# Mask parts in one run of fetches, and loads and sources issued in another order, in a two-layer graph-attention kernel

## The chip, the cores and the metric

One Trainium2 chip, of which one core runs the kernel. The metric is the time of one execution on the device, in microseconds (us); lower is better. Engines: TensorE (PE; its weight loads are PEld), VectorE (DVE), ScalarE (ACT), GpSimd (POOL), and SyncE (SP), which here only issues DMA transfers.

## The reference, cut to what matters

`x` is (8, 2048, 256) in float32, `adj` (2048, 2048) of 0 and 1 in int32. Two layers, each with a residual:

```
h = relu(layernorm(x))
q, k, v = h Wq^T + bq, h Wk^T + bk, h Wv^T + bv        # 4 heads of 64
s = clip(q k^T / 8, -10, 10); s = where(adj == 0, -10, s)
a = softmax of s within each chunk of 256 keys (8 chunks)
x = x + layernorm(sum over the chunks of a v, times Wo^T, + bo + h) * gamma + beta

h = relu(layernorm(x));  q = h W                       # 4 heads of 64
e = leaky_relu(q a_src [row] + q a_dst [column], 0.2)
x = x + elu(softmax(where(adj > 0, e, -9e15)) q)       # over all 2048 columns
```

## The kernel before, in words

**Layer 0** runs over 256 steps: 8 batches, 4 blocks of 512 queries, 8 chunks of 256 keys (the loop at line 731; its counter stands in `here[0]`). A step has two key tiles. Its contexts (line 460) take the weights that were made two steps before; its scores (line 440 on PE) are those of two steps ahead. DVE clips and masks a score tile (line 448, with `limit`, which holds the mask), ACT takes the exponential (line 454), POOL adds the two key tiles (line 725), and PE adds up over the keys (line 471). The sums then go a long way: ACT copies them (line 478), SP spreads them over the partitions by a DMA (line 480), DVE takes the reciprocal (line 485), SP writes it to memory and reads it back four times (lines 487 and 490), and DVE multiplies the contexts by it (line 498). POOL adds that to what earlier chunks gave (line 500).

**The order is written out by hand.** Each engine runs its instructions in the order of the program, and SP's queue is in order too: a transfer whose buffer isn't free holds up whatever stands behind it. In a step the program has: the first half of the contexts, the first `advance()`, four score tiles (the exponentials of the first two after them), the sums of the next step, their copy and its DMA, the other exponentials and POOL's additions, the second half of the contexts, the accumulation, the reciprocal with its DMAs, and the second `advance()`.

`aside` is a list of generators that hold all other work in pieces. `advance()` (line 212) goes through the list: a generator that yields `True` or `False` lets the next one have its turn, one that yields `None` has done a heavy piece, and the call ends there. Before step 0 such a generator also goes to the end of the list. `later()` (line 198) yields `False` until `here[0]` has grown. `drain(until)` calls `advance` until a condition holds. `quiet` has generators that `tick` moves in every round: `finish` (line 502: output projection, second layernorm, and the DMA of the result to memory from POOL's queue, line 553) and the statistics of the next batch.

**The mask** comes in 32 parts: 4 query blocks, 4 row tiles each, 2 halves of 1024 columns. For a part, SP loads 128 x 1024 int32 (line 251; three buffers `adj_in`), ACT casts it to bfloat16 (line 257), DVE takes the smallest value (line 258), PE transposes it in eight (line 272), and DVE makes `limit` of it (line 273). `make_limit(qb)` (line 244) does the eight parts of one query block, with three fetches at its start; `other_limits` runs it for blocks 1, 2 and 3 and joins `aside` at step 0. Scores of a block can't be issued before its mask is there (line 714), so a block that is not done is made in a `drain`. The rest of `aside` at that time is the first batch: `batch` and `block` (turning h by PE transposes, lines 144 to 164, and projections to k, v and q with PE at line 153).

**The change of layers.** `last_batch` makes batch 7 of layer 0, then runs `sources_of` (line 567) and `preparation(0)` (line 588), both in `aside`, while layer 0 still works on its last batch. `sources_of` multiplies W by the two attention vectors: four times a product on POOL (line 579) and its sum on DVE (line 583), with a `yield True` between. `preparation(b)` loads the four blocks of `x1` (the result of layer 0, in memory; line 110 through `ahead`), one ahead of use, makes h, turns it, gets the attention terms `er` (line 606), writes them to memory (line 622) with their extremes (`ends`, line 624), reads the extremes of all partitions back (`gm`, line 626), and later makes the projection qn.

**Layer 1** has 32 passes (8 batches, 2 pairs of heads, 2 halves of the rows) of 16 rounds (the loop at line 903; `here[0]` grows once in four rounds). At the start of a pass ACT makes `near` (line 798) from `es`, two rows that `sources` (line 779) reads back from memory with a DMA to all partitions; DVE makes e (line 809), PE the products (line 820) and sums (line 832), ACT and POOL pair the tiles for the sums (lines 924 and 928). `es` of the next pass is loaded in round 2 or 8; that of the first pass after the `drain` at line 890, right ahead of the loop. Preparation of the next batch and the `ending` of a pass run in `aside`.

Of the kernel before, what the change touches and what calls it, by code (L numbers as in the profile page):

```python
# [16 lines left out]
P = 128  # L17
# [34 lines left out]
def layers(  # L52
# [54 lines left out]

    def load(rows, blk):
        xb = big.tile([P, NT, F], F32, tag="x", name="x", bufs=3)
        nc.sync.dma_start(xb, rows[blk * QB : (blk + 1) * QB, :].rearrange("(t p) f -> p t f", p=P))  # L110
        return xb

    def ahead(rows):

        coming = load(rows, 0)
        for blk in range(NQB):
            xb = coming
            if blk + 1 < NQB:
                coming = load(rows, blk + 1)
            yield xb  # L120
# [77 lines left out]
    def later():  # L198
        n = here[0]
        while here[0] < n + 1:  # L200
            yield False
# [9 lines left out]

    def advance(all_of=True):

        moved = all_of and tick()
        for steps_of in list(aside):
            got = next(steps_of, aside)
            if got is aside:
                aside.remove(steps_of)
            moved = moved or got is not False
            if got is None:  # L220
                if here[0] < 0:
                    aside.append(aside.pop(aside.index(steps_of)))
                break
        return moved
# [18 lines left out]

    def make_limit(qb):
        parts = [(t, half) for t in range(NT) for half in range(2)]

        def fetch(k):
            t, half = parts[k]
            q0 = qb * QB + t * P
            raw = adj_in[(qb * len(parts) + k) % 3]  # L250
            nc.sync.dma_start(raw, adj[q0 : q0 + P, half * 1024 : (half + 1) * 1024])
            return raw

        def cast(k):

            m = masks[:, k % 2, :]
            nc.scalar.copy(m, raws[k])
            nc.vector.tensor_reduce(
                below[:, qb, k : k + 1], raws[k], mybir.AxisListType.X, ALU.min
            )  # L260
            return m
# [4 lines left out]
        yield True  # L266
        for k, (t, half) in enumerate(parts):
            if k + 3 < len(parts):
# [8 lines left out]
            if k + 1 < len(parts):  # L277
                m = cast(k + 1)
            else:
                made.append(qb)  # L280
            yield

    def other_limits():
        for qb in range(1, NQB):
            yield from make_limit(qb)

# [92 lines left out]

    first_batch, first_limit = batch(0), make_limit(0)  # L380
    next(first_batch)
# [4 lines left out]
    for name, w in (("q", Wq), ("k", Wk), ("v", Wv), ("o", Wo)):  # L386
        raw = big.tile([P, FC, F], F32, tag="c", name="w_raw")
        nc.sync.dma_start(raw, w.rearrange("(c p) f -> p c f", p=P))
        if name == "k":
            next(first_limit)  # L390
        if name == "o":
# [169 lines left out]

    shared = {}
    moments = const.tile([P, B, NKT, 2], F32, tag="moments", name="moments")
# [3 lines left out]
    def sources_of(W, a):  # L567
# [8 lines left out]
        for ic in range(FC):  # L576
            for s in range(2):
# [3 lines left out]
                )  # L581
                yield True
                nc.vector.tensor_reduce(
                    wa[:, ic, H * s : H * s + H], prod, mybir.AxisListType.X, ALU.add
                )
        shared["w"], shared["wa"] = w, wa

    def preparation(b):
# [8 lines left out]
        hTs = []  # L597
        for blk, xb in enumerate(ahead(x1[b])):
            if blk == 0:
# [23 lines left out]
        bounds = dram.tile([P, 2], F32, tag=f"ends{b}", name=f"ends{b}")  # L623
        nc.sync.dma_start(bounds, ends)
        gm = big.tile([P, P, 2], F32, tag="h", name="gm", bufs=3)
        nc.sync.dma_start(
# [37 lines left out]
        nc.scalar.copy(for_sums, bcast(share[:, :, 1, :], 3, 32))  # L664
        yield True

        while b == 0 and here[0] < (B - 1) * NQB * NCH + 3 * NCH + 4:
# [35 lines left out]
    steps = [(b, qb, c) for b in range(B) for qb in range(NQB) for c in range(NCH)]  # L703
    aside += [first_batch, first_limit]
    for _ in range(6):
# [25 lines left out]
    for n in range(-2, len(steps)):  # L731
        here[0] = n
        if n >= 0:
            b, qb, c = steps[n]
            if n == 0:
                aside.append(other_limits())
            b1 = 1 if n == 1 else b + 2 if (qb, c) == (NQB - 1, NCH - 2) else B
# [33 lines left out]
        if n < NQB * NCH or used[0] == 0 or qb == NQB - 1 or qb == 0 and c < NCH // 2:  # L771
            advance()
        else:
            tick()


    inverse_most = const.tile([P, 4 * B], F32, tag="most", name="most")

    def sources(held, hp, half):

        es = []
        for hh in range(2):
            e = big.tile([P, HALF], F32, tag="add", name="es")
            nc.sync.dma_start(
                e,
                held[2 * hp + hh, 2 * half : 2 * half + 2, :, :]
                .rearrange("b c p -> (b c p)")
                .partition_broadcast(P),
            )
            es.append(e)  # L790
        return es

# [97 lines left out]
    drain(lambda: 0 in shared)  # L890
    following, near = {0: sources(shared[0][1], 0, 0)}, []

# [10 lines left out]
    for s, (k, jt) in enumerate(rounds):  # L903
# [10 lines left out]
        if jt == (2 if k % 4 < 3 else 8) and k + 1 < len(passes):  # L914
            b1, hp1, half1 = passes[k + 1]
            drain(lambda: b1 in shared)
            following[k + 1] = sources(shared[b1][1], hp1, half1)
        weigh_rows(jt, hp, now, qn, acc)
# [334 lines left out]
```

## Time and profile before

| what | value |
|---|---|
| median of 3 runs | 4297.43 us (4297.36 to 4297.71) |
| the profiled execution | 4298.93 us, its span 4297.1 us |
| mean granted TensorE clock | 0.991 of full speed |
| layer 0 / layer 1 | to about 2780 us / from there |
| 32 mask parts made | casts, minima and `limit` from 18.0 to 299.9 us |
| DMA moved | 248.16 MB, 58 GB/s on average |

The profile shows one execution. Busy time is counted by engine; "idle before" is the time an engine waited ahead of an instruction, and the arrow names what ended that wait. The granted clock says what share of full speed the chip allowed TensorE at that time. SP's rows are the time that its queue spent on issuing transfers, waits between them included.

### The profile page before, as it was taken

What the parts mean: (1) busy time and instruction counts of PE and PEld (TensorE: products, weight loads), DVE (VectorE), ACT (ScalarE), POOL (GpSimd) and SP (SyncE); (2) the same over time, 40 slices, a digit from 0 to 9 for tenths busy, and PEclk for the clock granted to TensorE, in tenths of its full rate; (3) what the DMA queues carried; (4) which work ended last, traced back from release to release, by engine and by line L of the source; (5) the groups of instructions that cost most, each with busy time, mean ns of one, the idle gap of its engine ahead of it and who ended that gap; (6) DMA issues with size and microseconds to landing.
All of it is one profiled execution on the core that took longest, in us unless ns stands there. A gap on an engine that the chain in (4) does not pass through costs nothing. (4 is left out here: it accounts for less than half of the span.)

```text
span 4297.1 us, 86491 instructions
## 1 busy us (share of the span) xinstructions
PE 4103.1 (95%) x34742; PEld 1452.8 (34%) x34742; DVE 3221.3 (75%) x3974; ACT 2527.1 (59%) x3194; POOL 3409.1 (79%) x1795
## 2 busy tenths in 40 slices
PE   7889999999999999999999999989999999999998
PEld 3333333333333333333333333323333233333322
DVE  4676766666667666666666567689898898988997
ACT  4555555555655565555555567565666656566665
POOL 2467787887788788788788778878887888887897
PEclk9999999999999999999999999999999999999999
DMA  3221121122112111112211121211221212122121
GB/s 100 81 90 49 47 59 57 47 55 60 47 54 62 49 52 54 57 47 54 61 49 52 59 61 46 86 57 52 60 70 33 75 52 67 53 59 70 33 62 34
DMA packets 280267, 248.16 MB, mean 58 GB/s; under 512 B 95792, under 2 KB 230704, under 8 KB 279856
## 3 DMA queue, kind: packets, MB, share of 16 engines
q1 hardware_dynamic: 275248, 225.76, 18.7%
q0 software_dynamic: 4608, 16.78, 1.0%
q8 instruction: 275, 4.51, 0.5%
q14 instruction: 136, 1.11, 0.1%
HBM read 204.15 MB, written 36.18 MB: 56 GB/s over the span
## 5 line engine op out<-in xcount | busy, mean ns | idle before, releaser
L448 DVE SCALAR_TENSOR_TENSOR E<-big,limit 128x1024 f32<-128x1024 f32 x1024 | 1182.7, 1217 | 653.3 <-PE big L440 647.1
L725 POOL TENSOR_TENSOR add<-E 128x1024 f32<-128x1024 f32 x512 | 1203.5, 2372 | 569.8 <-PE both L460 474.2
L454 ACT ACTIVATE E<-E 128x1024 f32<-128x1024 f32 x1024 | 1055.0, 1057 | 540.3 <-DVE E L448 521.9
L809 DVE SCALAR_TENSOR_TENSOR e<-big,far,limit 128x1024 f32<-128x1024 f32 x1024 | 1239.6, 1275 | 39.5 <-POOL t L928 18.3
L928 POOL TENSOR_TENSOR t<-t,e 128x1024 f32<-128x1024 f32 x448 | 1055.2, 2388 | 226.7 <-ACT t L924 225.6
L820 PE MATMUL acc<-e,qn 128*32 128x512 f32 x8192 | 1035.6, 596 | 5.6 <-DVE e L809 5.5
L440 PE MATMUL big<-qT,kT 64*128 64x512 f32 x4096 | 966.8, 609 | 43.0 <-DVE E L448 35.6
L460 PE MATMUL both<-E,v 128*32 128x512 f32 x8192 | 991.9, 596 | 0.5 <-DVE c L498 0.2
L924 ACT ACTIVATE t<-e,quot 128x1024 f32<-128x1024 f32 x512 | 561.4, 1142 | 267.9 <-PE big L832 165.0
L440 PEld LDWEIGHTS big<-qT,kT 64*128 64x128 f32 x4096 | 366.3, 187 | 589.9 <-issue 384.1
L500 POOL TENSOR_TENSOR acc<-acc,c 128x1024 f32<-128x1024 f32 x224 | 530.3, 2368 | 1.4 <-DVE c L498 1.4
L460 PEld LDWEIGHTS both<-E,v 128*32 128x32 f32 x8192 | 274.9, 110 | 601.8 <-issue 345.7
L820 PEld LDWEIGHTS acc<-e,qn 128*32 128x32 f32 x8192 | 274.5, 110 | 504.8 <-issue 462.0
L832 PE MATMUL big<-t,for_sums 128*32 128x512 f32 x2048 | 359.3, 596 | 62.3 <-POOL t L928 51.1
L498 DVE TENSOR_TENSOR c<-both,r 128x512 f32<-128x512 f32 x448 | 308.8, 690 | 44.3 <-PE both L460 17.3
L471 PE MATMUL big<-add,ones 128*32 128x512 f32 x2048 | 282.7, 610 | 12.2 <-DVE E L448 1.8
L478 ACT COPY s<-big 128x512 f32<-128x512 f32 x256 | 150.1, 586 | 81.2 <-PE big L471 81.1
L832 PEld LDWEIGHTS big<-t,for_sums 128*32 128x32 f32 x2048 | 76.2, 109 | 282.2 <-POOL t L928 172.2
L164 ACT COPY hT<-big 128x512 f32<-128x512 f32 x128 | 74.2, 580 | 135.2 <-PE big L156 135.2
L144 ACT ACTIVATE h<-x,off,rstd 128x256 f32<-128x256 f32 x256 | 139.1, 592 | 4.7 <-POOL off L135 4.7
L337 ACT ACTIVATE qT<-big,bq 128x512 f32<-128x512 f32 x64 | 44.0, 687 | 153.9 <-PE big L153 153.9
L318 ACT COPY v<-big 128x512 f32<-128x512 f32 x64 | 37.4, 584 | 157.4 <-PE big L153 120.1
(116 smaller groups left out, 3122.3 us busy)
## 6 DMA issues: line engine op xcount, KB each, us to landing
r<-inv SPq DMA_DIRECT2D x1024, 64.0 KB
x<-in_x_dram SPq DMA_DIRECT2D x96, 512.0 KB
es<-er SPq DMA_DIRECT2D x64, 512.0 KB
adj_in<-in_adj_dram SPq DMA_DIRECT2D x32, 512.0 KB
x<-o POOLq DMA_DIRECT2D x32, 512.0 KB, 3.3
x<-x SPq DMA_DIRECT2D x32, 512.0 KB
xh<-x SPq DMA_DIRECT2D x64, 256.0 KB
out_dram<-xh SPq DMA_DIRECT2D x64, 256.0 KB
```

What stands on the lines that cost most here:

```text
L440: nc.tensor.matmul(ps[:, hh, :], ks[kt // NT][own, hp, (kt % NT) * P : (kt % NT + 1) * P], qs[qb][own, hp, :], start=True, stop=True,)
L448: nc.vector.scalar_tensor_tensor(e, ps, -0.5, bcast(limit[:, qb, kt, :], 1, 2), ALU.max, ALU.min)
L454: nc.scalar.activation(e, e, AF.Exp, scale=0.25 * EDGE)
L460: nc.tensor.matmul(both[part][32 * h : 32 * h + 32, :], vs[kt // NT][:, kt % NT, mine], es[h // 2][:, h % 2, :], start=first, stop=not first,)
L498: nc.vector.tensor_tensor(to[:, part, :], both[part], r, ALU.mult)
L500: nc.gpsimd.tensor_tensor(acc, acc, to, ALU.add)
L725: nc.gpsimd.tensor_tensor(both, tiles[0][hp], tiles[1][hp], ALU.add)
L809: nc.vector.scalar_tensor_tensor(e, near[hh], far[:, jt, h : h + 1], limit[:, 2 * half : 2 * half + 2, jt, :], ALU.max, ALU.min,)
L820: nc.tensor.matmul(acc[blk][32 * q : 32 * q + 32, :], qn[jt // NT][:, jt % NT, hp * P + 32 * q : hp * P + 32 * q + 32], es[q // 2][:, blk, :],
L832: nc.tensor.matmul(den[32 * q : 32 * q + 32, :], for_sums[:, m, 2 * hp + q // 2, :], ts[q // 2][:, q % 2, :], start=(m == 0 and k == 0), s ...
L924: nc.scalar.activation(t, now[hh], AF.Copy, scale=quot[:, jt // 2, h : h + 1])
L928: nc.gpsimd.tensor_tensor(ts[hh], ts[hh], now[hh], ALU.add)
```

## The change

There are four edits to the program's order. None changes what is computed.

- **One generator for the mask.** `limits` replaces `make_limit` and `other_limits`. It runs over all 32 parts; each is fetched three ahead of its use, also over the border of a query block. Before step 0 it stops once block 0 is made. From step 0 on it goes to the end of `aside`; in the second `advance` of steps 0 to 7 (`mask_first`) it gets its turn ahead of the others.
- **Queue of the first loads of layer 1's input.** `load` and `ahead` take a queue. The four `x1` loads of `preparation(0)` are issued by POOL (`nc.gpsimd`), those of the later batches by SP, as before.
- **Two waits for the next step.** In `sources_of`, `yield from later()` stands between product and sum in place of `yield True`. In `preparation`, for every batch, one stands between the DMA that writes `ends` and the one that reads `gm`.
- **Sources of the first pass.** `sources` is defined earlier and takes tag and number of buffers. `es` of pass 0 is loaded within `preparation(0)`, after `for_sums`, in buffers of the tag "q"; the later ones where they were, in the tag "add".

```diff
@@ -105,18 +105,18 @@
     def heads_tile(name, tag, bufs=2):
         return big.tile([P, 2, QB], F32, tag=tag, name=name, bufs=bufs)
 
-    def load(rows, blk):
+    def load(rows, blk, queue=nc.sync):
         xb = big.tile([P, NT, F], F32, tag="x", name="x", bufs=3)
-        nc.sync.dma_start(xb, rows[blk * QB : (blk + 1) * QB, :].rearrange("(t p) f -> p t f", p=P))
+        queue.dma_start(xb, rows[blk * QB : (blk + 1) * QB, :].rearrange("(t p) f -> p t f", p=P))
         return xb
 
-    def ahead(rows):
-
-        coming = load(rows, 0)
+    def ahead(rows, queue):
+
+        coming = load(rows, 0, queue)
         for blk in range(NQB):
             xb = coming
             if blk + 1 < NQB:
-                coming = load(rows, blk + 1)
+                coming = load(rows, blk + 1, queue)
             yield xb
 
     power = const.tile([P, 1], F32, tag="power", name="power")
@@ -209,10 +209,10 @@
             moved = moved or got is not False
         return moved
 
-    def advance(all_of=True):
+    def advance(all_of=True, mask_first=False):
 
         moved = all_of and tick()
-        for steps_of in list(aside):
+        for steps_of in sorted(aside, key=lambda steps_of: mask_first and steps_of is not all_limits):
             got = next(steps_of, aside)
             if got is aside:
                 aside.remove(steps_of)
@@ -241,13 +241,14 @@
     adj_in = [big.tile([P, 1024], I32, tag="kv", name="adj_in", bufs=12) for _ in range(3)]
     masks = big.tile([P, 2, 1024], BF16, tag="kv", name="masks", bufs=12)
 
-    def make_limit(qb):
-        parts = [(t, half) for t in range(NT) for half in range(2)]
+    def limits():
+
+        parts = [(qb, t, half) for qb in range(NQB) for t in range(NT) for half in range(2)]
 
         def fetch(k):
-            t, half = parts[k]
+            qb, t, half = parts[k]
             q0 = qb * QB + t * P
-            raw = adj_in[(qb * len(parts) + k) % 3]
+            raw = adj_in[k % 3]
             nc.sync.dma_start(raw, adj[q0 : q0 + P, half * 1024 : (half + 1) * 1024])
             return raw
 
@@ -255,8 +256,9 @@
 
             m = masks[:, k % 2, :]
             nc.scalar.copy(m, raws[k])
+            qb, t, half = parts[k]
             nc.vector.tensor_reduce(
-                below[:, qb, k : k + 1], raws[k], mybir.AxisListType.X, ALU.min
+                below[:, qb, 2 * t + half : 2 * t + half + 1], raws[k], mybir.AxisListType.X, ALU.min
             )
             return m
 
@@ -264,7 +266,7 @@
         yield True
         m = cast(0)
         yield True
-        for k, (t, half) in enumerate(parts):
+        for k, (qb, t, half) in enumerate(parts):
             if k + 3 < len(parts):
                 raws.append(fetch(k + 3))
             ps = aux(BF16).rearrange("p (k q) -> p k q", q=P)
@@ -276,13 +278,11 @@
             )
             if k + 1 < len(parts):
                 m = cast(k + 1)
-            else:
+            if (t, half) == (NT - 1, 1):
                 made.append(qb)
             yield
-
-    def other_limits():
-        for qb in range(1, NQB):
-            yield from make_limit(qb)
+            while here[0] < 0 and made:
+                yield False
 
     qkv, norm_of = {}, {}
 
@@ -377,7 +377,7 @@
                 yield False
             yield from block(b, blk, ready[blk], turned, *qkv[b])
 
-    first_batch, first_limit = batch(0), make_limit(0)
+    first_batch, all_limits = batch(0), limits()
     next(first_batch)
     for _ in range(2):
         next(quiet[0])
@@ -387,7 +387,7 @@
         raw = big.tile([P, FC, F], F32, tag="c", name="w_raw")
         nc.sync.dma_start(raw, w.rearrange("(c p) f -> p c f", p=P))
         if name == "k":
-            next(first_limit)
+            next(all_limits)
         if name == "o":
 
             got = big.tile([P, FC, F], F32, tag="c", name="w_halves")
@@ -559,7 +559,7 @@
         yield True
 
 
-    shared = {}
+    shared, following, near = {}, {}, []
     moments = const.tile([P, B, NKT, 2], F32, tag="moments", name="moments")
     least = const.tile([P, B, H], F32, tag="least", name="least")
     spans = const.tile([P, B, 2 * H], F32, tag="spans", name="spans")
@@ -579,11 +579,25 @@
                 nc.gpsimd.tensor_tensor(
                     prod, w[:, ic, :].rearrange("p (h d) -> p h d", h=H), bcast(a_sb[:, s, :], 1, H), ALU.mult
                 )
-                yield True
+                yield from later()
                 nc.vector.tensor_reduce(
                     wa[:, ic, H * s : H * s + H], prod, mybir.AxisListType.X, ALU.add
                 )
         shared["w"], shared["wa"] = w, wa
+
+    def sources(held, hp, half, **place):
+
+        es = []
+        for hh in range(2):
+            e = big.tile([P, HALF], F32, name="es", **place)
+            nc.sync.dma_start(
+                e,
+                held[2 * hp + hh, 2 * half : 2 * half + 2, :, :]
+                .rearrange("b c p -> (b c p)")
+                .partition_broadcast(P),
+            )
+            es.append(e)
+        return es
 
     def preparation(b):
 
@@ -595,7 +609,7 @@
 
         er = const.tile([P, NQB, P], F32, tag="wv", name="er")
         hTs = []
-        for blk, xb in enumerate(ahead(x1[b])):
+        for blk, xb in enumerate(ahead(x1[b], nc.sync if b else nc.gpsimd)):
             if blk == 0:
                 yield True
             hT = big.tile([P, FC, QB], F32, tag="kv", name="hT1", bufs=12)
@@ -622,6 +636,7 @@
             nc.sync.dma_start(held[:, :, c, :], er[32 * c : 32 * c + 2 * H, :, :])
         bounds = dram.tile([P, 2], F32, tag=f"ends{b}", name=f"ends{b}")
         nc.sync.dma_start(bounds, ends)
+        yield from later()
         gm = big.tile([P, P, 2], F32, tag="h", name="gm", bufs=3)
         nc.sync.dma_start(
             gm.rearrange("p k s -> p (k s)"), bounds.rearrange("k s -> (k s)").partition_broadcast(P)
@@ -663,6 +678,8 @@
         for_sums = big.tile([P, NKT // 2, H, 32], F32, tag="o", name="for_sums")
         nc.scalar.copy(for_sums, bcast(share[:, :, 1, :], 3, 32))
         yield True
+        if b == 0:
+            following[0] = sources(held, 0, 0, tag="q", bufs=4)
 
         while b == 0 and here[0] < (B - 1) * NQB * NCH + 3 * NCH + 4:
             yield False
@@ -701,7 +718,7 @@
 
 
     steps = [(b, qb, c) for b in range(B) for qb in range(NQB) for c in range(NCH)]
-    aside += [first_batch, first_limit]
+    aside += [first_batch, all_limits]
     for _ in range(6):
         advance()
     aside.append(bias())
@@ -733,7 +750,7 @@
         if n >= 0:
             b, qb, c = steps[n]
             if n == 0:
-                aside.append(other_limits())
+                aside.sort(key=lambda steps_of: steps_of is all_limits)
             b1 = 1 if n == 1 else b + 2 if (qb, c) == (NQB - 1, NCH - 2) else B
             if b1 < B:
                 aside.append(batch(b1) if b1 + 1 < B else last_batch())
@@ -769,26 +786,12 @@
         if inside:
             r = spread(got)
         if n < NQB * NCH or used[0] == 0 or qb == NQB - 1 or qb == 0 and c < NCH // 2:
-            advance()
+            advance(mask_first=0 <= n < NCH)
         else:
             tick()
 
 
     inverse_most = const.tile([P, 4 * B], F32, tag="most", name="most")
-
-    def sources(held, hp, half):
-
-        es = []
-        for hh in range(2):
-            e = big.tile([P, HALF], F32, tag="add", name="es")
-            nc.sync.dma_start(
-                e,
-                held[2 * hp + hh, 2 * half : 2 * half + 2, :, :]
-                .rearrange("b c p -> (b c p)")
-                .partition_broadcast(P),
-            )
-            es.append(e)
-        return es
 
     def nears(es, hp, off_s):
         got = []
@@ -888,7 +891,6 @@
     passes = [(b, hp, half) for b in range(B) for hp in range(2) for half in range(2)]
     rounds = [(k, jt) for k in range(len(passes)) for jt in range(NKT)]
     drain(lambda: 0 in shared)
-    following, near = {0: sources(shared[0][1], 0, 0)}, []
 
     def begun(k, jt):
 
@@ -914,7 +916,7 @@
         if jt == (2 if k % 4 < 3 else 8) and k + 1 < len(passes):
             b1, hp1, half1 = passes[k + 1]
             drain(lambda: b1 in shared)
-            following[k + 1] = sources(shared[b1][1], hp1, half1)
+            following[k + 1] = sources(shared[b1][1], hp1, half1, tag="add")
         weigh_rows(jt, hp, now, qn, acc)
         if jt % 2 == 0:
             ts = []
```

## The prediction, made before the changed kernel was run

> **What bounds the kernel now.** First the engine totals and the 40 slices, then the stretches by window, then TensorE's (PE's) own timeline for each stretch whose sum falls short, then the timeline of the engine named as releaser, back to a queue.
>
> ```profile
> span 4297.1 us, 86491 instructions
> PE 4103.1 (95%) x34742; PEld 1452.8 (34%) x34742; DVE 3221.3 (75%) x3974; ACT 2527.1 (59%) x3194; POOL 3409.1 (79%) x1795
> ...
> PE   7889999999999999999999999989999999999998
> ```
>
> PE is busy 95%; the slices that fall short are the first three and the one at the change of layers. By windows (columns: start:end, length, busy and count of PE, PEld, DVE, ACT, POOL, then granted clock, DMA share, GB/s):
>
> ```profile
> 60.00:150.00 90.00, 83.83 (x724) 32.04 (x728) 43.09 (x61) 48.11 (x63) 42.26 (x25) 0.98 0.16 49
> 150.00:200.00 50.00, 34.45 (x242) 14.29 (x236) 34.62 (x34) 22.95 (x27) 17.42 (x9) 0.80 0.31 100
> 200.00:300.00 100.00, 83.96 (x630) 30.14 (x628) 85.40 (x103) 53.54 (x62) 63.98 (x34) 0.95 0.34 107
> 300.00:2440.00 2140.00, 2118.80 (x16966) 766.96 (x16968) 1457.15 (x2118) 1239.04 (x1566) 1733.84 (x929) 1.00 0.19 53
> 2440.00:2640.00 200.00, 179.94 (x1310) 62.54 (x1300) 129.25 (x177) 116.25 (x150) 162.42 (x84) 0.95 0.23 62
> ```
>
> From 300 to 2440 us PE is busy 99%: nothing can be won there. 150 to 300 and 2440 to 2640 lose 31.6 and 20.1 us and run at a lower clock. The change touches these two. PE's timeline gives the single losses (start, length, the idle time before it in brackets and its releaser):
>
> ```profile
> 161.74 1.04 PE L272 MATMUL big<-identb,masks 128*128 128x128 bf16 x8 [2.24 <-ACT masks L257]
> ...
> 188.00 3.79 PE L440 MATMUL big<-qT,kT 64*128 64x512 f32 x8 [5.63 <-ACT hT L164]
> ...
> 253.37 2.08 PE L440 MATMUL big<-qT,kT 64*128 64x512 f32 x4 [6.40 <-DVE E L448]
> ```
>
> **Opening.** A bare step of layer 0 takes PE 8.47 us (its sums L471 start at 2666.25 and again at 2674.72; rows there: sums 1.06, contexts 3.84, scores 3.70, ends overlapping). To each idle time I add what the matmuls behind it took beyond such rows at full clock.
> - (a) At step 7 eight parts are made in one burst, 153.72 to 170.29: 16.57 us. PE needs 0.55 a part (at full clock a row of L272 starts at 271.02 and the matmul after it at 271.57), 4.4; the scores behind it take 4.93 against 3.70. Loss 12.2 + 1.2 = 13.4.
> - (b) Three new fetches, part 0 first: idle 5.63, scores 3.79 against 1.85, sums 1.81 against 1.06. Loss 8.3.
> - (c) The next restart of fetches: idle 6.40, scores 2.08 against 1.13, sums 1.94 against 1.06, then 0.49 of contexts. Loss 8.7.
>
> The cause of (b) and (c) is the landing of the part that was just asked for. VectorE (DVE) waits for it behind ScalarE's (ACT's) cast, and PE behind both:
>
> ```profile
> 186.36 1.22 DVE L258 TENSOR_REDUCE below<-adj_in 128x1 int32<-128x1024 int32 x1 [7.33 <-DMA adj_in<-in_adj_dram]
> ...
> 250.96 1.22 DVE L258 TENSOR_REDUCE below<-adj_in 128x1 int32<-128x1024 int32 x1 [5.91 <-DMA adj_in<-in_adj_dram]
> ```
>
> With one generator over all 32 parts no fetch is asked for later than three parts ahead, so (b) and (c) go, and the issue order of the changed program shows no burst: 24 parts stand one or two to a step from step 2 to 15. Steps 2 to 8 take nine of them beside projections. There DVE has 6.36 us of its own (4.62 for four score tiles, 1.49 products, 0.25 reciprocal) and 2.34 for a part (1.21 + 1.13), 8.7; PE has 8.47 + 1.85 for a projection piece + 0.55, 10.9. So DVE stays below PE and I cost the parts at PE's 0.55, which both kernels pay. Were that cover gone, each would cost its 2.34.
> - (d) Seven steps carry two parts, not eight. DVE then needs 6.36 + 4.68 = 11.0, and such a step takes 10.85 (sums at 268.31 and 279.16), against PE's 8.47 + 1.10 = 9.57. One fewer: -1.3.
> - (e) A cast (1.04 on ACT) now stands between the two hT copies of a turn in two steps. Bounds 0 and 2.1; I take 1.0, by the row.
> - Three more fetches before step 0: DMA share is 0.39 in the first 60 us and PE waits there for other things: 0, bounds 0 and 2.
>
> What is late next: ACT's hT copy, then PE itself. Opening: -13.4 - 8.3 - 8.7 - 1.3 + 1.0 = **-30.7**, between -18 (the burst's clock stays low and half of (b) returns at another landing) and -37.
>
> On the clock, the burst's row comes first: no gap in it is over 2.24 us, and yet 160 to 170 us has a granted clock of 0.50. The Trainium skill, "TensorE: Matmul & The Clock Gate", Part 1, has the half clock only after an idle window of about 3.4 us; by it, 3.5 us of (a) would not be due to the gaps and would stay, and this sum would be -27.2. The row decides here.
>
> **Change of layers.** Five losses, found the same way:
>
> ```profile
> 2471.08 2.08 PE L440 MATMUL big<-qT,kT 64*128 64x512 f32 x4 [8.29 <-DVE E L448]
> ...
> 2564.62 2.08 PE L440 MATMUL big<-qT,kT 64*128 64x512 f32 x4 [5.14 <-DVE E L448]
> ...
> 2625.92 1.13 PE L440 MATMUL big<-qT,kT 64*128 64x512 f32 x4 [3.77 <-DVE E L448]
> ```
>
> - A (8.29 idle and 2.7 of slow clock behind it): DVE's first reduce L583 waits 10.17 us for POOL's product L579. The added wait for the next step stands between the two. But the issue order shows that the first product already was in the second advance of one step and its reduce in the first advance of the next; the order about them is unchanged. **I cost the removal of A at nothing.**
> - B (1.44): the later products now have a step before their reduces. -1.4.
> - C: the x1 load of line 110 waits on SP until POOL has let go of its buffer. The sums' copy L480 is queued behind it, and DVE's reciprocal behind that; the rows below show both. Idle 5.14, then 0.95 + 0.87 + 0.24 slow. With the loads on POOL's queue SP is free: -7.2.
> - D: gm's load L626 waits on SP for ends to land in memory, with the same two behind it (reciprocal idle 6.33). It is now issued a step later, when ends has landed (3.3 us). Idle 3.77 + 0.87 + 1.0: -5.6.
> - E: at 2785.20 PE waits 4.63 for e, since ACT L798 waits 11.66 for es. The changed order issues es(0) five steps after gm, well before the layer's end. DVE's L809 waits 2.45 + 0.61 for it: -3.1; the rest of the idle time is DVE's own first tiles.
>
> ```profile
> 2555.29 0.38 SPq L110 DMA_DIRECT2D x<-x  x1
> 2555.77 0.55 SPq L480 DMA_DIRECT2D sum<-s  x1
> ...
> 2561.11 0.25 DVE L485 RECIPROCAL sum<-sum 128x16 f32<-128x16 f32 x1 [6.68 <-DMA sum<-s]
> ```
>
> What this costs: four loads issued by POOL. Before has no load on that queue, but 32 stores, 0.84 us each (0.967 at most). Below: 0, if POOL has slack (162.42 busy of 200). Above: 4 x 0.84 = 3.4 on the path, since POOL is full in places (38.16 of 40 us in 2520 to 2560) and its adds free the tiles that DVE writes. I take 3.4. The issue order shows nothing that these loads wait for but stores long done; behind them stand the pairwise adds L725 and, through them, the sums L471. Layers: -1.4 - 7.2 - 5.6 - 3.1 + 3.4 = **-13.9**.
>
> A transfer that VectorE can hold up is the Trainium skill's rule against this edit ("DMA: Bandwidth & Descriptors", SWDGE vs HWDGE vs iDMA): GpSimd writes the descriptors of its own DMAs itself and can be locked out by VectorE, so plain transfers belong on SP or ACT. The 32 stores between 837 and 967 ns, with DVE 75% busy, show no such lockout; what it would cost is rival 1.
>
> **Layer 1.** The added wait also shifts the preparation of batches 1 to 7 by up to four rounds each. In before, DVE waits for gm 8.5 us in all, and PE only some 0.2 each time. I take 0; bounds -8.5 (all of it on the path) and +9 (seven turn-overs of pieces into a fuller round, 1.3 each, one L809).
>
> **Sum.** -30.7 - 13.9 = -44.6. The profiled execution took 4298.93 (span 4297.1 and 1.8 around it): 4254.3. The median of the runs is 1.5 below it: **4253**.
>
> **Rivals.**
> 1. POOL becomes the bound at the change of layers: each of the four issues is held for the length of DVE's score group (4.62) and not 0.84, 4 x 3.78 = 15 more: 4268. For it: 38.16 of 40 busy. Against: the stores' even 0.84. 14%. The skill's rule above is this case.
> 2. The nine parts of steps 2 to 8 are not hidden, since the transposes take one of three PSUM pairs that scores use and DVE frees it late: 9 x 2.34 = 21: 4274. For it: the double steps do follow DVE (10.85 against 11.0). Against: 8.7 below 10.9 here. 10%.
> 3. A goes too, because the new rhythm ahead of it lets POOL reach the product earlier: -11: 4242. For it: A is POOL's lateness, not a dependency. Against: unchanged order. 8%.
> 4. The change doesn't do what it says (the landing of fetches still ends last, as a part is used three parts after its fetch, and four loads are only late elsewhere): 4297. 3%.
> 5. Slower: a fetch on SP waits until DVE's reduce has freed its buffer, with the sums' copy queued behind it, as in C. It decides if the reduce ends after the copy is due. Price 7.2 in each of 14 steps, 101 against 45 won: 4354. Against: the reduce stands ahead of the four score tiles (4.62 us) on DVE, and before's double steps have the same order without such a wait. 5%.
>
> **Numbers.** Forecast 60%, in 4243 to 4265; the rivals' chances as given. 4236 to 4276 takes in the forecast and rivals 1 to 3 with the bounds of layer 1, and leaves out 4, 5 and what falls outside by several bounds together, near 2 in 10. A measurement of this kernel tells 0.2% (8.6 us) from no change. Faster by more than that: forecast and rivals 1 to 3, 92%; within it: rival 4, 3%; slower: rival 5, 5%.
>
> **What would show it.** Right: in the changed profile 150 to 300 us has no idle time over 2 us ahead of L440, L272 stands alone or in twos, SP has no fetch that waits over 3 us; at the change of layers DVE's reciprocal has no wait of 6 us, E's 11.66 is gone, and A is still there with about 8 us. Wrong: PE idle behind L273 in steps 2 to 8 (rival 2), POOL issues over 2 us (rival 1), SP's fetches ahead of late sums (rival 5), or losses in 300 to 450 us from batch 1, whose turn now starts some six steps later.

## The result, and the profile after

Before: 4297.43 us (median of 7 runs, 4295.62 to 4298.41). After: 4283.12 us (7 runs, 4280.82 to 4285.06). The ratio is 0.9967, with a 95% interval of 0.9957 to 0.9977: the changed kernel is faster by 14.3 us, 0.33%. The forecast was 44.6 us. The profiled execution of the changed kernel took 4285.06 us, its span is 4283.3, so 13.8 us less than that of before.

The page of the changed kernel. It has 50 instructions more; among the engines only POOL has more, four (the loads):

```profile
span 4283.3 us, 86541 instructions
PE 4101.6 (96%) x34742; PEld 1478.7 (35%) x34742; DVE 3220.3 (75%) x3974; ACT 2528.9 (59%) x3194; POOL 3411.4 (80%) x1799
...
PE   7999999999999999999999989999999999999998
```

The first slices have filled; the one at the change of layers has not. The same windows again for the two stretches that the change touches (150 to 300 held 118.41 us of PE work before, 2440 to 2640 held 179.94):

```profile
150.00:300.00 150.00, 137.20 (x1081) 49.13 (x1073) 127.01 (x156) 85.76 (x100) 104.69 (x52) 0.99 0.30 93
2440.00:2640.00 200.00, 179.25 (x1328) 63.64 (x1331) 132.88 (x184) 121.89 (x156) 160.38 (x87) 0.94 0.19 58
```

Windows of equal time don't hold equal work. To see where the 14 us came from I take the start of each step's copy of the sums (line 478, one to a step) and the end of each pass in layer 1 (the copy dT), and subtract the two kernels:

| stretch | forecast | measured |
|---|---|---|
| layer 0 up to step 226 | -30.7 | -26.0 |
| from there to the end of layer 1's second pass | -13.9 | +0.9 |
| the rest of layer 1 and the end | 0 | +11.3 |
| span | -44.6 | -13.8 |

Midway, at step 26, the difference is -37.3. That isn't all won: at step 30, where it is -37.6, before had issued 64 more projection matmuls for k and q than after (1.85 us for 16) and 64 more for v (1.9 us for 32). These are about 11 us of work that after does later, so some 26 are won.

**Change of layers.** PE's timeline has A as it was, B and C are gone, D is down from 3.77 to 2.64 us, and there are two new losses:

```profile
2446.60 2.08 PE L440 MATMUL big<-qT,kT 64*128 64x512 f32 x4 [8.28 <-DVE E L448]
...
2497.07 1.18 PE L156 MATMUL big<-ident,h 128*128 128x128 f32 x4 [6.69 <-ACT h L144]
...
2504.76 1.18 PE L156 MATMUL big<-ident,h 128*128 128x128 f32 x4 [3.68 <-ACT h L144]
```

PE waits for h. What h waited for stands in ACT's timeline, and why that came late in POOL's:

```profile
2496.42 1.09 ACT L144 ACTIVATE h<-x,off,rstd 128x256 f32<-128x256 f32 x2 [13.82 <-DMA x<-x]
2497.41 1.99 ACT L454 ACTIVATE E<-E 128x1024 f32<-128x1024 f32 x2
2499.31 0.56 ACT L478 COPY s<-big 128x512 f32<-128x512 f32 x1
```

```profile
2487.51 2.40 POOL L500 TENSOR_TENSOR acc<-acc,c 128x1024 f32<-128x1024 f32 x1
2489.99 0.23 POOL L132 TENSOR_SCALAR rstd<-mv 128x4 f32<-128x4 f32 x1
2490.30 1.04 POOL L133 TENSOR_TENSOR rstd<-rstd,power 128x4 f32<-128x4 f32 x1
2491.40 0.23 POOL L134 TENSOR_SCALAR off<-mv 128x4 f32<-128x4 f32 x1
2491.72 0.20 POOL L135 TENSOR_TENSOR off<-off,rstd 128x4 f32<-128x4 f32 x1
2492.22 1.59 POOL L110 DMA_DIRECT2D x<-x  x2 [0.30 <-issue]
2500.91 4.65 POOL L742 TENSOR_TENSOR add<-E 128x1024 f32<-128x1024 f32 x2 [7.09 <-ACT E L454]
```

Read them from the bottom. The two loads stand behind POOL's additions, its accumulation and the roots of `finish`; they are issued at 2492.22, and h runs when the first lands, at 2496.42. Behind h on ACT stand the exponentials and the copy of the sums, so POOL's next additions wait 7.09 us for ACT, and DVE's reciprocal waits 10.61 for the sums:

```profile
2501.73 0.25 DVE L485 RECIPROCAL sum<-sum 128x16 f32<-128x16 f32 x1 [10.61 <-DMA sum<-s]
```

Steps 229 and 230 together end 15.2 us later against before than step 228 did. In before SP issued the two loads 9.2 us ahead of h, and h waited for POOL's roots, not for a load (SP's and ACT's timelines):

```profile
2492.17 0.97 SPq L110 DMA_DIRECT2D x<-x  x2
```

```profile
2501.34 1.09 ACT L144 ACTIVATE h<-x,off,rstd 128x256 f32<-128x256 f32 x2 [4.28 <-POOL off L135]
```

**Layer 1.** Batches 1 to 6 take 186.9 us each in before (one 187.1) and 189.0 in after.

### The profile page after: what moved, and what is told of

It is laid out like the page before. It is cut to its first block, busy times and chain, and to the rows that moved or that the text cites. A ratio compares the mean times of both kernels' runs of the same rounds, so it can differ in the third digit from the quotient of the medians.

```text
span 4283.3 us, 86541 instructions
## 1 busy us (share of the span) xinstructions
PE 4101.6 (96%) x34742; PEld 1478.7 (35%) x34742; DVE 3220.3 (75%) x3974; ACT 2528.9 (59%) x3194; POOL 3411.4 (80%) x1799
## 5 line engine op out<-in xcount | busy, mean ns | idle before, releaser
L823 PE MATMUL acc<-e,qn 128*32 128x512 f32 x8192 | 1065.2, 595 | 3.5 <-DVE e L812 3.4
L823 PEld LDWEIGHTS acc<-e,qn 128*32 128x32 f32 x8192 | 292.1, 110 | 496.2 <-issue 435.4
L835 PE MATMUL big<-t,for_sums 128*32 128x512 f32 x2048 | 380.3, 596 | 66.7 <-POOL t L930 50.1
L498 DVE TENSOR_TENSOR c<-both,r 128x512 f32<-128x512 f32 x448 | 308.8, 689 | 40.2 <-PE both L460 14.3
L153 PE MATMUL big<-w,hT 128*32 128x256 f32 x2048 | 151.1, 380 | 4.1 <-ACT dT L944 4.1
L144 ACT ACTIVATE h<-x,off,rstd 128x256 f32<-128x256 f32 x256 | 139.1, 592 | 14.2 <-DMA x<-x 13.8
```

The source lines that it names most:

```text
L498: nc.vector.tensor_tensor(to[:, part, :], both[part], r, ALU.mult)
L823: nc.tensor.matmul(acc[blk][32 * q : 32 * q + 32, :], qn[jt // NT][:, jt % NT, hp * P + 32 * q : hp * P + 32 * q + 32], es[q // 2][:, blk, :],
L835: nc.tensor.matmul(den[32 * q : 32 * q + 32, :], for_sums[:, m, 2 * hp + q // 2, :], ts[q // 2][:, q % 2, :], start=(m == 0 and k == 0), s ...
```

## The experiments

16 kernels in four sets; each time is a median, with before at 4297 to 4298 in each set. Theories are named as in the expectations.

**1. The opening alone.** The changed kernel with the other edits undone:

```diff
-        for blk, xb in enumerate(ahead(x1[b], nc.sync if b else nc.gpsimd)):
+        for blk, xb in enumerate(ahead(x1[b], nc.sync)):
...
-                yield from later()    # ahead of the sum of the product
+                yield True
...
-        yield from later()            # ahead of gm
...
+    following[0] = sources(shared[0][1], 0, 0, tag="add")   # behind the drain again
```

> The one generator for the mask, without the three edits at the change of layers. Theory O (the opening's gain is lasting, and what looks like more at step 26 is projection work of batch 1 that is done later): the starts of the sums' copies show 26.0 us won at equal work (step 226), so 4297.4 - 26.0 = 4271.4, between 4268 and 4275. Rival (the opening's gain is given back within layer 0 or at the change of layers, whatever the other edits are): about the changed kernel's 14 us, 4283.

4272.52 us, ratio 0.9935 (0.9922 to 0.9949). Theory O holds: the opening alone wins 25.9 us, more than the whole change. What stands at the change of layers and in layer 1 costs 10.6 us net.

**2. The x1 loads back on SP** (only the first pair of lines of the diff above).

> The changed kernel with the four x1 loads of batch 0 back on SP. Theory Q (the first load stands behind POOL's additions and roots, and PE's 6.69 + 3.68 us of idle time and the slow clock after them come from that): the 15 us of steps 229 and 230 go and stall C (7.2 us) comes back, 4283.1 - 15 + 7.2 = 4275.3. Rival R (these 15 us come from the other edits, the roots or the later preparation; POOL's queue is innocent): stall C comes back and nothing goes, 4290.

4278.71 us. Less is won than theory Q gave, 4.4 us and not 7.8, and by another sum: C did not come back, and of the 15.2 us at steps 229 and 230 8.3 stayed (28.8 us ahead at step 226, 30.3 at 228, 22.1 at 230). So POOL's queue is 6.9 of the 15.2, and 8.3 has another cause. These are steps of one execution each, but the same stall is 14.8 to 15.1 us in experiments 3, 6 and 14, which have the loads on POOL too, and 8.0 in experiment 7, with them on SP. What PE loses here is the second turn, since its h stands behind the exponentials on ACT:

```profile
2495.68 1.18 PE L156 MATMUL big<-ident,h 128*128 128x128 f32 x4 [4.91 <-ACT h L144]
```

**3 and 4. The wait ahead of gm**, for batch 0 alone in the changed kernel, and for batches 1 to 7 alone in before.

```diff
+        if b == 0:          # experiment 4, in before: if b:
             yield from later()
         gm = big.tile([P, P, 2], F32, tag="h", name="gm", bufs=3)
```

> The changed kernel with the added wait ahead of gm in batch 0 alone; batches 1 to 7 issue gm right after ends, as before. Theory S (the 12.3 us that layer 1 loses, 2.05 in each of batches 1 to 6, come from the preparation that is shifted by that wait): layer 1 is as long as before from its second batch on, 4283.1 - 12.3 = 4270.8. Rival T (layer 1 is slower for another reason, such as the buffers of es in the first pass or where the layer starts): 4283, no change.

> The kernel before with one edit alone: the wait ahead of gm in batches 1 to 7 (not in batch 0). Theory S: 2.05 us more in each of batches 1 to 6, 4297.4 + 12.3 = 4309.7. Rival T: 4297, or up to 8.5 us less if DVE's waits for gm were on the path.

4272.98 and 4312.40 us: 10.1 less than the changed kernel, 14.0 more than before (ratio 1.0032, 1.0020 to 1.0044). Theory S holds from both sides. In experiment 3 a batch takes 186.9 us again, in experiment 4 it takes 189.0.

**5. What the 8.3 us are: the wait behind the product undone** (`yield True` there, all else as in the changed kernel).

> The changed kernel with the wait between product and sum undone (a plain turn, as before), loads still on POOL. Theory V (that wait shifts all of the preparation by about a step, to a slot where h stands ahead of the exponentials on ACT; 8.3 of the 15 us come from that, the rest from the load's place in POOL's queue): 4283.1 - 8.3 + 2 (stall B) = 4277, between 4274 and 4280. Rival W (the wait has no part in it): 4283.1 + 1.5 = 4284.6.

4275.37 us, 7.7 less: theory V. The wait ahead of each sum moves all of the preparation, and the first turn of h with it, to another place in its step. Without it, the second h follows on ACT right behind the first turn, and the exponentials come after (in the changed kernel two groups of them stand between):

```profile
2477.39 1.09 ACT L144 ACTIVATE h<-x,off,rstd 128x256 f32<-128x256 f32 x2 [8.69 <-DMA x<-x]
2479.26 0.58 ACT L164 COPY hT<-big 128x512 f32<-128x512 f32 x1 [0.78 <-PE big L156]
2479.74 1.09 ACT L144 ACTIVATE h<-x,off,rstd 128x256 f32<-128x256 f32 x2
```

The first h still waits for its load, and PE 5.07 us for that h, which fits the part of POOL's queue; no run undoes both together.

**6 and 7. A step between the loads and h**, first tried with a wait alone, with the loads on POOL and on SP (gm wait in batch 0 alone).

```diff
             if blk == 0:
-                yield True
+                yield from later() if b == 0 else (True,)
```

> The changed kernel with the gm wait in batch 0 alone (4273.0 as measured), and with one wait for the next step more: between the issue of the first x1 load of batch 0, still by POOL, and the first h that needs it. Theory Q (the 15 us of steps 229 and 230 are h waiting on ACT for a load issued 4 us before, with the exponentials and the sums' copy queued behind it): the load has landed a step before, the stall goes, 4273.0 - 15 = 4258, between 4255 and 4262. Rival P (POOL is the bound there or its transfers are held up, whatever their lead): 4270 to 4273.

> The kernel of the run above with the four loads on SP in place of POOL. Theory Q: the queue matters only through the time of issue; with a step between, 4258 as well if stall C (a load that waits on SP for its buffer) stays away as it did with the loads on SP in the changed kernel, 4265 if it comes back. Rival P: POOL's share was the cost, so some 7 to 15 us less than with the loads on POOL.

4271.07 and 4265.70 us. The first is the same as experiment 3 (4272.98), and it had to be: the order of instructions is the same on every engine. `later()` started in a step's second advance ends in the next step's first, where a plain turn ends too. It says nothing about Q, and that the second meets Q's 4265 is luck: C, which that number has in it, did not come back. It repeats experiment 2 (5.4 less on SP). It is the same trap as stall A, which the change wanted to remove with the same wait.

**8 and 9. A whole step between them**, `later()` and then a plain turn.

> What the earlier kernel with a wait before h was to be: that wait turned out to change no engine's order, since a wait for the next step that starts in a step's second advance ends in the next one, as a plain turn does. Here a plain turn stands behind the wait, so that the first h really comes a step after the loads (still POOL's), with the gm wait in batch 0 alone. Theory Q (h on ACT waits for a load issued 4 us before, exponentials and the sums' copy behind it): the 15 us of steps 229 and 230 go, 4272 - 15 = 4257, up to 4260. Rival P (POOL is late there by itself, with the roots' 3.7 us and two issues ahead of its additions): some 6 of the 15 stay, 4263, or all of it, 4272.

> The kernel of the run above with the four loads on SP. Theory Q: the lead hides the queue, within 2 us of the run above. Rival P: two issues less ahead of POOL's additions (1.6 us) and what they delay, 2 to 5 us less than the run above; if stall C returns on SP, 7 more.

4263.53 and 4268.71 us. On POOL 7.5 to 9.5 us are won: half of the 15, as rival P had it (4263), not all of it. The step between gave the loads no lead, since POOL came to them no sooner than before: they are issued at 2492.48, h waits for them until 2497.20, and PE for h:

```profile
2497.85 1.18 PE L156 MATMUL big<-ident,h 128*128 128x128 f32 x4 [5.30 <-ACT h L144]
```

On SP the stall at the turn is down to 2.28 us, but C is back (5.35 us): with another lead the load of the third block meets its buffer still in use.

**10 and 11. The sum of the product half a step later**, loads on POOL and on SP (as in experiment 3 for gm).

```diff
                 yield from later()
+                yield True
                 nc.vector.tensor_reduce(
```

> The kernel of the first run of this set with each sum of the attention product half a step later still: in the second advance of the next step. Theory A (stall A is DVE's sum standing ahead of the score tiles while POOL is late with the product, and the change left that order as it was): 8.3 idle and some 2.7 us of slow clock go, 4258 - 11 = 4247, between 4244 and 4251. Rival B (POOL is behind at that point, and the idle time only moves to the next instruction that needs it): 4255 to 4258.

> The kernel with the sums of the attention product half a step later (4253.3, its trace still shows PE waiting 3.14 and 1.25 us for POOL's additions behind roots and two load issues) with the loads on SP. Theory P (the issues on POOL delay the additions): 1.6 to 4 us less, 4250. Rival C (a load on SP waits for its buffer again and holds up the sums): 7 more, 4260.

4253.28 and 4261.47 us. The first lies in neither range: both started from a 4258 for experiment 6, which measured 4271.07. By the place of the gain theory A holds, and the kernel wins more than A: 17.8 against experiment 6, 10.3 of it at step 225, where A was. DVE's sum now finds its product ready (no idle time stands before it):

```profile
2445.24 0.39 DVE L584 TENSOR_REDUCE wa<-prod 128x4 f32<-128x256 f32 x1
```

The rest comes with the shift: the first h now stands in another place, and steps 229 and 230 lose 5.7 us against before and not 14.8. Experiment 10 also keeps the added wait of experiment 6, and 11 does not. Here that wait does change the order on ACT (the second h comes behind the exponentials), so the two differ by more than the queue. With the loads on SP rival C holds all the same, by its rows. SP's and PE's timelines of that kernel show the load for the third block waiting, the sums' copy behind it, and PE at the end of the chain:

```profile
2519.49 0.38 SPq L110 DMA_DIRECT2D x<-x  x1
2519.97 0.55 SPq L480 DMA_DIRECT2D sum<-s  x1
```

```profile
2528.58 2.08 PE L440 MATMUL big<-qT,kT 64*128 64x512 f32 x4 [5.17 <-DVE E L448]
```

**12. The roots apart from the loads**, in the kernel of experiment 11 (`later()` and a plain turn between the two).

> The kernel of the run above with a step between the roots on POOL and the first loads. Theory P (what is left at that place is the roots' time ahead of POOL's additions): no better than the run above, within 2 us. Rival L (h's wait for its load, 5.98 us on ACT, is what delays the exponentials): no gain either, as the lead of the load is the same; a difference over 3 us would speak against both.

4263.28 us: no gain, as both theories had it. C (5.06 us) is there again.

**13. What the runs point to**: late sums, roots apart, gm wait in batch 0 alone, the first two loads on SP, the other two on POOL.

```diff
-        coming = load(rows, 0, queue)
+        coming = load(rows, 0, first or queue)
...
-                coming = load(rows, blk + 1, queue)
+                coming = load(rows, blk + 1, first if first and blk == 0 else queue)
...
-        for blk, xb in enumerate(ahead(x1[b], nc.sync if b else nc.gpsimd)):
+        for blk, xb in enumerate(ahead(x1[b], nc.sync if b else nc.gpsimd, nc.sync)):
```

> Late sums of the product, gm wait in batch 0 alone, a step between roots and loads, the first two x1 loads on SP (their buffers are free) and the other two on POOL (on SP they bring stall C back). Theory: the roots apart save 1 to 2 us against the kernel with late sums and all loads on POOL (4253.3), stall C stays away: 4252, between 4248 and 4255. Rival (the gain is taken by where layer 0's own small stalls fall, 2 to 4 us either way): 4250 to 4257, not to be told from 4253.

4252.34 us, ratio 0.9894 (0.9879 to 0.9909): the fastest kernel here, 30.8 us under the changed one. It can't be told from experiment 10. C is gone; at the first turn PE still waits 1.20 and 1.25 us for POOL's additions.

**14 and 15. Why the wait ahead of gm costs.**

```diff
-        for _ in range(3):
+        for _ in range(0 if b else 3):    # 14, in the changed kernel
+        for _ in range(8 if b else 3):    # 15, in before
             yield True
```

> The changed kernel, with the gm wait in all batches, but for batches 1 to 7 the three plain turns between gm's load and its first use left out, so that the projection qn comes some 2 rounds later than in before, not 5. Theory S1 (layer 1 loses since the last qn pieces cross into the next pass): all of them stay within their pass, 4283.1 - 12 = 4271, up to 4275. Theory S2 (a separate step between ends and gm is itself what costs, wherever qn falls): 4283.

> The kernel before with eight plain turns in place of three behind gm's load in batches 1 to 7: gm is issued right after ends, and only what follows is 5 rounds later. Theory S1: the shift alone costs what the gm wait cost, 4297.4 + 12 to 14 = 4309 to 4312. Theory S2: 4297.

4271.34 and 4306.99 us: with the wait but without the shift nothing is lost (186.9 us a batch), and with the shift alone 9.4 us are (188.6 a batch). S1 holds in kind: between ends and gm the wait itself is free. Its size does not: 9.4 is less than the 12 to 14 that it gave. DVE's timeline of the changed kernel shows the last qn of a batch, with a pass ended at 3297.83 (the copy dT, line 944):

```profile
3293.54 0.69 DVE L693 TENSOR_TENSOR qn<-big,share 128x512 f32<-128x512 f32 x1 [0.40 <-PE big L153]
3300.54 0.69 DVE L693 TENSOR_TENSOR qn<-big,share 128x512 f32<-128x512 f32 x1 [3.93 <-ACT t L926]
```

In before all eight were done 10.7 us ahead of that copy (the projection for batch 3, at the end of pass 10). The last projection now runs at the change of passes, where the ending's transposes and the first tiles of the next pass want PE and DVE, too. It does so for batches 2 to 7, which are prepared while batches 1 to 6 run. Batch 1's preparation is shifted as well, but its last qn (2907.91) stays 13.1 us ahead of the copy dT, and batch 0, during which it runs, loses nothing: the lead is 25.1 us after its second pass and 25.0 after its fourth. So it is the crossing that costs. But its price does not go by the number of pieces: in experiment 15 three of the eight cross and a batch loses 1.7 us, in the changed kernel one crosses and it loses 2.05. In what the 2.05 us go was not taken apart.

**16. The opening without its mixing**: experiment 1 with a plain `advance()` in the second place.

> The opening's change alone (4272.5), without the turn that the mask gets ahead of the others in the second advance of steps 0 to 7. Its order has one mask part in step 3 or 4, one or two more and then a burst of six at step 7, and no restart of fetches. Theory O1 (the burst's loss of 13.4 for eight parts is idle time and slow clock for each part, the restarts' 17 are a separate loss that the single generator takes away): 6/8 of the burst's loss comes back, 4272.5 + 10 = 4282.5. Rival O2 (three fetches ahead are enough, and the burst costs nothing when parts are already fetched): 4272.5 to 4275.

4284.95 us, 12.4 more than with the mixing. O1 holds against O2, but the 12.4 can't all be put to the burst. In the two profiled executions, 9.6 us apart, this kernel is 8.2 us behind that of experiment 1 at step 8, right after a burst of six parts: 1.4 a part, where the prediction's 13.4 for eight had 1.7. By step 17, when all parts are made, 2.6 of it are made up, and 4.1 more are lost by step 226, most of them between steps 100 and 120; no run takes that apart. PE's timeline and the clock by 5-us windows (the last three columns: granted clock, DMA share, GB/s):

```profile
156.95 1.03 PE L274 MATMUL big<-identb,masks 128*128 128x128 bf16 x8 [1.75 <-ACT masks L258]
159.70 1.03 PE L274 MATMUL big<-identb,masks 128*128 128x128 bf16 x8 [1.72 <-ACT masks L258]
162.70 1.03 PE L274 MATMUL big<-identb,masks 128*128 128x128 bf16 x8 [1.97 <-ACT masks L258]
```

```profile
155.00:160.00 5.00, 1.53 (x16) 1.09 (x14) 5.00 (x5) 2.09 (x2) 0.00 (x0) 0.67 0.62 208
160.00:165.00 5.00, 3.03 (x19) 2.06 (x19) 5.00 (x6) 1.82 (x2) 0.00 (x0) 0.50 0.74 217
```

The parts were fetched three ahead; DVE is busy all the time with its two operations for each (2.34 us), and PE, at 1.53 and 3.03 of 5 us, waits on the chain behind it and slows down as well.

## Why the prediction was wrong, point by point

The table's three stretches share the 30.8 us that are missing from the forecast: 4.7 in the opening, 14.8 at the change of layers, 11.3 in layer 1. Two steps of the prediction failed at the change of layers, and one in layer 1.

- **Opening, -30.7: right in kind, too large by 4.7.** Its signs came true: from 150 to 300 us no idle time of PE is over 1.46 us, and no fetch of a part takes SP over 1.66. At step 8 the lead over before is 21.4 us, where (a) + (b) gave 21.7. At step 17, with all parts made in both kernels, it is 29.0; 1.3 of these are eight transposes of h that before had done by then and after had not (0.66 us for four). So (c) + (d) + (e) brought some 6.3 us and not 9.0, and 1.7 more are lost from there to step 226. One piece of that is where the last lines of the prediction looked: from step 17 to step 47 or so, where batch 1 is turned and projected, idle times before PE add up to 4.95 us in after and 1.76 in before. Steps 8 to 17 bring 7.6 us here, and 7.6 to 9.1 in experiments 1, 3, 6 and 10, which have the same order there; what comes later scatters by as much as the whole shortfall (last section), so its split is not exact.
- **A at nothing, B, C, E: right.** A is 8.28 us in after, and -10.3 when its order really changes. After step 228 come -6.2 at step 234 (C, forecast -7.2), -4.5 at step 240 (D, -5.6; the four er transfers, 2.86 us on SP, still stand ahead of the sums' copy; 3.3 are lost again between steps 241 and 244, which was not taken apart), -2.9 in the first pass (E, -3.1).
- **"I take 3.4" for the loads on POOL: this step failed.** It asked what POOL's issues do to what stands behind them on POOL. It did not ask what stands ahead of them and who is waiting for the data: the loads left SP, where they would be issued at once, and went behind 4.7 + 2.4 us of additions and the roots. "The issue order shows nothing that these loads wait for" is true of semaphores and says nothing of a queue. It cost 6.9 us (experiment 2).
- **The wait behind the product at "-1.4": the same failure.** I saw that later products have a step before their sums, and costed the saving. That the wait moves all that follows it in the same generator, h above all, to where h stands ahead of ACT's exponentials, was left out: 8.3 us (experiment 2's rest), 7.7 (experiment 5).
- **"Layer 1: I take 0; bounds -8.5 and +9": failed.** It measured +12.3 over batches 1 to 6, outside even the bound, since the shift carries the last projection of each preparation into the next pass (experiments 3, 4, 14 and 15). DVE's waits for gm did go, and were worth nothing to PE. The bound had seven turn-overs of one L809 (1.3 each); it is six of 2.05.
- **The rivals.** Rival 1 named the place and, by chance, the price (15 us), but not the mechanism: no issue on POOL was held. Two took 1.59 us, and h started 4.2 us after the first was issued. So the Trainium skill's rule ("DMA: Bandwidth & Descriptors", SWDGE vs HWDGE vs iDMA: plain transfers from SP or ACT) gave the right direction for the first two loads (experiment 2), though no row shows VectorE holding POOL up: each of the four issues took 0.76 to 0.83 us. For the third it gave the wrong one in three kernels, where on SP it brought C back (5.1 to 5.4 us of PE's time); in experiments 2 and 7 it did not. The others did not occur: the parts of steps 2 to 8 were hidden as forecast (rival 2; the lead at step 8 above), A stayed (3), the opening's losses went (4), and no fetch took SP over 1.66 us (5).
- **The clock.** Experiment 16 repeats what the prediction weighed: no gap in its burst is over 1.97 us, and the granted clock is 0.50. Here the rows speak against the Trainium skill's idle window of about 3.4 us ("TensorE: Matmul & The Clock Gate", Part 1) as the only way to the half clock; the word "only" is the prediction's.

## What to carry to other kernels

Where an order is written out by hand, a wait put into a chain moves everything behind it: ask where each later piece lands in its step and what it then stands ahead of, down to the end of the chain. For a load that changes queues, price what is ahead of it there and how soon its data is needed, not only the issue itself; a load that may block on its buffer belongs on a queue where nothing urgent is behind it, and one that is needed at once on the queue that is empty. And test whether a wait changes the order at all: here one "wait for the next step" out of two places did not.

## What the runs showed of the hardware that was not expected

- PE's granted clock drops to one half in a stretch of short gaps: 1.7 to 2.0 us each, with 1.0 us of work between them, 0.50 from 160 to 165 us (experiment 16).
- Kernels with the same layer 0 don't run it alike: in 14 profiled executions with the same order up to step 220 or so the lead over before at step 118 is between 23.0 and 28.9 us. So one execution of each does not tell a difference of some 4 us between two of these kernels, only medians do, and 10 and 13 are not told apart at all.
